# The third tile of x1n in blocks 2 to 6: turned by VectorE and memory, not by TensorE

## The chip, the core and the metric

The kernel runs on one core of one Trainium2 chip (trn2). A core has TensorE (matrix multiplications into PSUM), VectorE, ScalarE and GpSimd (elementwise work and sums), and SyncE, which here issues nearly all memory transfers. In the profile they are PE (its weight loads apart as PEld), DVE, ACT, POOL and SP. Each engine runs its own instructions in the order of the program; semaphores make one wait for another. Sixteen DMA engines carry the transfers.

The metric is the device time of one execution in microseconds (us), lower is better. A profiled execution gives a trace; its span runs from the first instruction to the last.

## The reference

A sandwich of two residual layers over x, 4 sequences of 1024 tokens with 512 features, all float32:

```python
x = x + _layernorm(_L0_attn_ref(_layernorm(x, axis=-1), Wq, Wv, Wo, Wg, ln_gamma, ln_beta, beta), axis=-1)
x = x + _layernorm(_L0_ffn_ref(_layernorm(x, axis=-1), gate_w, up_w, down_w, gate_s, up_s, down_s), axis=-1)
```

The first layer is a retention: q, v and g are projections of the normalised x (512 x 512 weights), v goes through a decaying running sum along the sequence, `out = q * ret` is normalised, scaled by `silu(g)` and projected by Wo. The second is a gated feed-forward layer with 1536 inner features, whose weights are rounded to 8-bit floats: `silu(x @ gate_w * gate_s) * (x @ up_w * up_s) @ down_w * down_s`.

Between the two stands what this change is about. x1 is x plus the first layer's normalised output; x1n is x1 normalised over its 512 features; the feed-forward layer reads x1n.

## The kernel before

**Blocks and tiles.** The 4096 tokens are cut into eight blocks (0 to 7) of 512, and a block into four tiles (s = 0 to 3) of 128 tokens. A tile has a token in each of the 128 partitions and 512 features beside each other. The feed-forward products sum over features, so for them features must lie in the partitions: each tile of x1n has to be turned (transposed). The turned block is x1nT, in two parts, because float32 values are carried as two numbers[...]: part 0 is the rounded value (`upper_of`, line 891, a copy on ACT), part 1 what is left (`rest_of`, line 894, a subtraction on VectorE).

**Two ways to turn a tile.** `turn_x1n` (875) has TensorE do it, four 128x128 pieces of a tile into one PSUM bank (`pt` in the profile). `move_x1n` (878) has VectorE turn 32x32 blocks (`xs`), writes these to DRAM in four stores of 64 KB (`mxs<-xs`) and returns a function that loads them back in exchanged places (`x1n<-mxs`, 256 KB), into the tile that x1n was in. In blocks 2 to 6, before the change, tiles 0 and 1 go through memory and tiles 2 and 3 through TensorE.

**The loop.** For block t the loop runs 12 steps (i = 0 to 11), one per 128 inner features: `f.gate(i)` and `f.up(i)` are eight matmuls each into a bank of the pair `pf` (`pfg`, `pfu`), `f.fuse(i)` multiplies the two on VectorE, and `f.down(i - 2)` sums into four banks (`pd`). Step 0's `f.gate(0)` is the first to read a block's x1nT; for its first chunk of features its first matmul reads part 0 of all four tiles and its second matmul part 1.

Into these steps the same loop weaves the first layer of later blocks: `f` is the feed-forward of block t, `b` the retention of block t + 1, `n` that of block t + 2, and `l` the feed-forward of block t - 1. `fast` holds from block 2 on for `b`. `n` exists for t = 1 to 5, so with `b` = blocks 2 to 6. In `b`'s last steps each tile goes through:

- `o_moments(s)`: mean and variance of the output projection in PSUM (`po`), VectorE; then the inverse root by GpSimd (`rstd_in_place`).
- `x1_of(s)` (852): three activations on ACT normalise it into x1n's tile, GpSimd adds it to x, SP stores the sum as `kept`.
- `x1_moments(s)` (863): the same statistics of x1; `x1n_of(s)` then normalises into x1n's tile.

Tiles 0 and 1 come early: x1_of in step 8, the moments and x1n in step 9. Tiles 2 and 3 have x1_of and their moments in step 10, and are turned in step 11.

**The projections of the next block.** `n.gap(...)` works off the passes of `n`'s v, q and g. Each pass multiplies by one 256 KB unit of weights from a ring of four (`w_ring`), and after a pass `fetch_weights` (418) has SP load the unit that comes four later. `n.gap(-2)` and `n.gap(-1)` in step 11 stand on both sides of the turns: the first starts v's chunk 0 (`begin`: two passes), the second ends it (the third pass, then a scan on VectorE) and starts chunk 1.

**What sets the order.** Every operation is issued through `InOrder` (67), which keeps the program's order on each engine; so in the profile nearly all work has line 75. SP's transfers stand in one queue, in the order of their calls. In the built program a transfer also waits for the one eight places before it on SP, as they share eight semaphores in turn.

Of the kernel before, what the change touches and what calls it, by code (L numbers as in the profile page):

```python
# [23 lines left out]
def sandwich(  # L24
# [298 lines left out]
    class Splitter:  # L323
# [34 lines left out]
        def load(self, k):  # L358

            w = wpool.tile([P, NC, D], F32R, tag=f"w{k}_sb", name=f"w{k}_units")  # L360
            for c in range(NC):
                sp.dma_start(w.bitcast(F32)[:, :, ts(c, P)], self.by_chunk(operands[k, c]["top"]))
            self.raw[k] = w
# [659 lines left out]
    b = Retention(1)  # L1023
# [177 lines left out]
    for t in range(NB):  # L1201
        f, n = Ffn(a), None
        fast = b is not None and b.fast
        for i in range(NI):
            if t > 0 and (t > 1 or i) and not (fast and i == 11):
                (f if i else l).rest((i - 1) % NI)
            if t == 0 and i == 0:
                n = Retention(2)

            if t > 0 and b and i == 0 and t < NB - 2:  # L1210
                n = Retention(t + 2)
# [81 lines left out]
                    n.diff_of(0)  # L1293
                    n.diff_of(1)
            if fast and i == 10:
                b.x1_of(2)
                b.x1_of(3)
            f.up(i)
            if n and i == 11:
                n.gap(-2)  # L1300
            if fast and i == 11:
                b.new_x1nT()
            f.fuse(i)
# [5 lines left out]
            if t == 0 and i == 9:  # L1309
                load = b.move_x1n(2)  # L1310
# [8 lines left out]
            if fast and i == 9:  # L1319
                b.o_moments(2)  # L1320
                loads = [b.move_x1n(s) for s in range(2)]
            if fast and i == 11:
                for s in range(2):
                    b.upper_of(s)
                    b.rest_of(s)
# [48 lines left out]
                n.diff_of(0)  # L1374
                n.diff_of(1)
            if fast and i == 10:
                b.x1_moments(2)
                b.x1_moments(3)
                b.x1n_of(2)
                if n:  # L1380
                    n.diff_of(2)
                    n.diff_of(3)
# [48 lines left out]
                f.down(NI - 2)  # L1431

            if n and i == 11:
                if t:
                    b.turn_x1n(2, "pf")
                    b.upper_of(2)
                    b.rest_of(2)
                b.turn_x1n(3, "pf")
                b.upper_of(3)
                b.rest_of(3)  # L1440
            if fast and i < 3:
                b.gap(3 * i + 2)
            if fast and i in (7, 8):
# [30 lines left out]
        l, a, b = f, b, n  # L1474
# [58 lines left out]
@with_exitstack  # L1533
def retention_ffn_sandwich(ctx: ExitStack, tc: tile.TileContext, *args):


    nc = tc.nc
    out, seq = args[-2:]
    kept = ctx.enter_context(tc.tile_pool(name="flag", bufs=1, space=bass.MemoryType.DRAM))
    flag = kept.tile([1, 1], I32, tag="flag", name="flag")  # L1540
    sandwich(tc, *args, flag=flag)
    beyond = nc.values_load(flag, min_val=0, max_val=0x7F800000)
    with tc.If(beyond != 0):
        with tc.tile_pool(name="rounded", bufs=1, space=bass.MemoryType.DRAM) as kept_rounded:
            weights = round_exactly(tc, kept_rounded, args[8:11], ("gate_w8", "up_w8", "down_w8"))
            sandwich(tc, *args[:8], *weights, *args[11:])
# [44 lines left out]
```

## Time and profile before

| | |
|---|---|
| median of 3 runs | 914.72 us (914.65 to 915.25) |
| the profiled execution, as a run | 913.0 us |
| its span | 911.2 us |
| VectorE busy | 631.3 us, 69% |
| ScalarE busy | 419.0 us, 46% |
| GpSimd busy | 241.4 us, 26% |
| transfers of SP's queue | 151.18 MB, 54.7% of what 16 DMA engines could be busy |
| granted clock of TensorE | 0.992 |

A busy share is an average over the span; what limits the kernel in one stretch is read from the timeline of that stretch. In the rows of a timeline stand the start, the length, the engine, the operation with what it writes and reads, and how many such instructions were merged; in square brackets, if there is one, the idle time before it and what ended it. A matmul's shown length holds its way through the array, so matmuls overlap: eight in a row begin 1.73 us after the eight before them. For a transfer the trace shows when SP issued it and how long it took to land.

### The profile page before, as it was taken

The page shows a single profiled execution, that of the slowest core. Times are in us where ns is not written, and L with a number is a line of the kernel's source. Part 1 is how long each engine was busy: PE and PEld are TensorE (multiplying, and loading weights), DVE is VectorE, ACT ScalarE, POOL GpSimd, SP SyncE. Part 2 cuts the span into 40 slices and gives each one's busy share as a digit, 9 for nine tenths or more (in the row PEclk, how much of TensorE's full clock was granted, in tenths as well). Part 3 has the DMA queues.
Part 4 walks back from the last instruction along what each step waited for, and adds up shares of the span by engine and source line. Part 5 has one row for each costly group of instructions (what it writes and reads, how often), then busy time and mean ns, then how long its engine had stood idle before and what let it go on. Part 6 is the DMA issues. An engine that isn't in the chain of part 4 may idle for free.

```text
span 911.2 us, 11999 instructions
## 1 busy us (share of the span) xinstructions
PE 884.0 (97%) x3948; PEld 741.0 (81%) x3948; DVE 631.3 (69%) x1071; ACT 419.0 (46%) x741; POOL 241.4 (26%) x304
## 2 busy tenths in 40 slices
PE   9999999989899999999999999999999999999995
PEld 7466777677688888888888888888888888888885
DVE  4888686667778684886668766786848855665545
ACT  1368556523454336443464534543364433644223
POOL 1214231301414214250332305142142503322030
PEclk9999999999999999999999999999999999999998
DMA  9964544666563775646745666627756464423021
GB/s 285 301 211 165 174 136 151 169 223 210 161 171 76 244 228 161 162 127 211 240 148 131 188 209 212 179 60 243 229 161 162 125 212 149 144 88 115 1 94 50
DMA packets 115579, 152.69 MB, mean 168 GB/s; under 512 B 10867, under 2 KB 54644, under 8 KB 115444
## 3 DMA queue, kind: packets, MB, share of 16 engines
q1 hardware_dynamic: 114644, 151.18, 54.7%
q10 hardware_dynamic: 864, 0.66, 0.3%
q8 instruction: 33, 0.54, 0.2%
q14 instruction: 38, 0.31, 0.1%
HBM read 117.46 MB, written 38.54 MB: 171 GB/s over the span
## 4 chain that ended last, share of the span: by engine, by line
PE 85%; DVE 7%; ACT 3%; DMA 2%; issue 1%; POOL 1%; DVEq 0%; SPq 0%; ACTq 0%; POOLq 0%
PE pfu L75 17%; PE pfg L75 16%; PE pd L75 15%; PE pg L75 9%; PE po L75 9%; PE pv L75 9%; PE pq L75 8%; DVE st L75 1%; DVE y L75 1%; PE idle L75 1%; DVE gate L75 1%; DMA x<-in_x 1%; PE var L75 1%; PE mu L75 1%; PE pt L75 1%
## 5 line engine op out<-in xcount | busy, mean ns | idle before, releaser
L75 PE MATMUL pfg<-x1nT,gate_sb 128*128 128x512 f32 x768 | 184.0, 382 | 1.6 <-ACT gate L75 1.5
L75 PE MATMUL pfu<-x1nT,up_sb 128*128 128x512 f32 x768 | 183.2, 381 | 0.9 <-DVE gate L75 0.9
L75 PE MATMUL pd<-down_sb,fuse 128*128 128x512 f32 x720 | 170.5, 379 | 0.0
L75 PEld LDWEIGHTS pfg<-x1nT,gate_sb 128*128 128x128 f32 x768 | 145.6, 191 | 24.8 <-ACT gate L75 3.9
L75 PEld LDWEIGHTS pfu<-x1nT,up_sb 128*128 128x128 f32 x768 | 145.0, 189 | 23.6 <-issue 1.9
L75 PEld LDWEIGHTS pd<-down_sb,fuse 128*128 128x128 f32 x720 | 141.3, 196 | 14.6
L75 ACT CAST fuse<-gate 128x512 fp32r<-128x512 f32 x90 | 55.6, 618 | 137.5 <-DVE gate L75 134.0
L75 DVE SCALAR_TENSOR_TENSOR gate<-pfu,us_sb,gate 128x512 f32<-128x512 f32 x96 | 71.7, 747 | 66.2 <-PE pfu L75 56.7
L75 ACT ACTIVATE gate<-pfg,gs_sb 128x512 f32<-128x512 f32 x96 | 65.6, 683 | 92.2 <-PE pfg L75 92.2
L75 POOL TENSOR_SCALAR mv<-mv 128x1 f32<-128x1 f32 (+1 forms) x82 | 23.0, 280 | 314.5 <-DVE mv L75 312.5
L75 DVE TENSOR_TENSOR fuse<-gate,fuse 128x512 fp32r<-128x512 f32 x90 | 71.0, 789 | 5.0 <-ACT fuse L75 4.8
L75 POOL TENSOR_TENSOR d<-d,x 128x512 f32<-128x512 f32 x28 | 41.7, 1511 | 89.6 <-ACT d L75 75.7
L75 DVE BATCH_NORM_STATS2 st<-x 128x6 f32<-128x512 f32 x64 | 43.6, 681 | 22.3 <-POOL x L75 17.3
L75 POOL TENSOR_TENSOR mv<-mv,nhalf 128x1 f32<-128x1 f32 (+1 forms) x75 | 52.2, 697 | 6.3
L75 POOL TENSOR_TENSOR x<-x,x1n 128x512 f32<-128x512 f32 x32 | 45.5, 1427 | 22.8 <-ACT x1n L75 15.8
L75 ACT ACTIVATE pv<-pv 128x512 f32<-128x512 f32 x28 | 16.3, 582 | 50.0 <-PE pv L75 50.0
L75 POOL TENSOR_TENSOR ysum<-y 128x512 f32<-128x512 f32 x8 | 10.6, 1324 | 105.1 <-DVE y L75 105.1
L75 POOL TENSOR_TENSOR sqsum<-sqsum,sq 128x512 f32<-128x512 f32 x24 | 33.7, 1404 | 17.4 <-ACT sq L75 10.1
L75 DVE TENSOR_TENSOR y<-pq,y 128x512 f32<-128x512 f32 x28 | 19.1, 682 | 22.7 <-PE pq L75 22.7
L75 DVE BATCH_NORM_STATS2 st<-po 128x6 f32<-128x512 f32 x32 | 21.9, 685 | 14.9 <-PE po L75 14.7
L75 DVE SCALAR_TENSOR_TENSOR y<-y,lnb_sb,mids 128x512 f32<-128x512 f32 x28 | 27.0, 965 | 7.1 <-ACT mids L75 7.0
L75 ACT ACT_TABLE_LOAD x19 | 24.4, 1283 | 16.3 <-DVE var L75 12.2
(214 smaller groups left out, 1488.9 us busy)
## 6 DMA issues: line engine op xcount, KB each, us to landing
x<-in_x SPq DMA_DIRECT2D x52, 256.0 KB, 5.4
kept<-x SPq DMA_DIRECT2D x32, 256.0 KB, 3.2
x<-kept SPq DMA_DIRECT2D x32, 256.0 KB, 4.3
out<-d SPq DMA_DIRECT2D x31, 256.0 KB, 2.0
w_ring<-dtop_v SPq DMA_DIRECT2D x24, 256.0 KB, 3.3
w_ring<-dlow_v SPq DMA_DIRECT2D x24, 256.0 KB, 3.4
w_ring<-ddiff_v SPq DMA_DIRECT2D x24, 256.0 KB, 3.5
w_ring<-dtop_q SPq DMA_DIRECT2D x24, 256.0 KB, 2.6
```

The source lines that it names most:

```text
L75: return lambda *args, **kwargs: tc.keep_in_program_order(op(*args, **kwargs))
```

## The change

In blocks 2 to 6 tile 2 takes the way of tiles 0 and 1. Its x1_of moves from step 10 to step 9, its x1_moments from behind `f.fuse(10)` to ahead of `f.up(10)`, and x1n_of(2) from behind x1_moments(3) to ahead of it; after that `move_x1n(2)` is called in step 10, and its load in step 11 behind `n.gap(-2)`. In step 11 tile 3 is now the only one that TensorE turns, and tile 2's upper_of and rest_of come after tile 3's. In block 7 (where there is no `n`) only x1n_of(2) changes places with x1_moments(3). No operation is new: all of them were in the kernel before for other tiles.

```diff
             if fast and i == 10:
-                b.x1_of(2)
+                if n:
+                    b.x1_moments(2)
+                else:
+                    b.x1_of(2)
                 b.x1_of(3)
             f.up(i)
             if n and i == 11:
                 n.gap(-2)
+                if t:
+                    load()
             if fast and i == 11:
                 b.new_x1nT()
             f.fuse(i)
...
             if fast and i == 9:
                 b.o_moments(2)
                 loads = [b.move_x1n(s) for s in range(2)]
+                if n:
+                    b.x1_of(2)
...
             if fast and i == 10:
-                b.x1_moments(2)
+                if not n:
+                    b.x1_moments(2)
+                b.x1n_of(2)
+                if n:
+                    load = b.move_x1n(2)
                 b.x1_moments(3)
-                b.x1n_of(2)
                 if n:
                     n.diff_of(2)
                     n.diff_of(3)
...
             if n and i == 11:
-                if t:
-                    b.turn_x1n(2, "pf")
-                    b.upper_of(2)
-                    b.rest_of(2)
                 b.turn_x1n(3, "pf")
                 b.upper_of(3)
                 b.rest_of(3)
+                if t:
+                    b.upper_of(2)
+                    b.rest_of(2)
```

## The prediction

> **What bounds the kernel now.** I read the page first, then TensorE's timeline around the turn of one block into the next, then SP's timeline over the same stretch, then what its transfers took to land.
>
> ```profile
> span 911.2 us, 11999 instructions
> PE 884.0 (97%) x3948; PEld 741.0 (81%) x3948; DVE 631.3 (69%) x1071; ACT 419.0 (46%) x741; POOL 241.4 (26%) x304
> PE 85%; DVE 7%; ACT 3%; DMA 2%; issue 1%; POOL 1%; DVEq 0%; SPq 0%; ACTq 0%; POOLq 0%
> ```
>
> TensorE is busy 97% of the span and is 85% of the chain that ended last. Each of its instructions that goes shortens the kernel, as long as TensorE finds its operands in time. So I need the slack of the operands at the place of the change. TensorE there (block 2, start and length in us):
>
> ```profile
> 303.38 1.89 PE L75 MATMUL pd<-down_sb,fuse 128*128 128x512 f32 x8
> 305.11 1.04 PE L75 MATMUL pt<-ident,x1n 128*128 128x128 f32 x8
> 305.90 1.11 PE L75 MATMUL pv<-diff,w_ring 128*128 128x512 f32 x4
> 306.85 1.03 PE L75 MATMUL pv<-xnT,w_ring 128*128 128x512 f32 x4
> 307.71 1.03 PE L75 MATMUL pv<-low,w_ring 128*128 128x512 f32 x4
> 308.57 1.89 PE L75 MATMUL pfg<-x1nT,gate_sb 128*128 128x512 f32 x8
> ```
>
> There is no gap. The eight `pt` are the turns of tiles 2 and 3. At 308.57 `pfg` starts: step 0 of the next Ffn and the first reader of all of x1nT. SP's issues over that stretch:
>
> ```profile
> 292.91 3.73 SPq L75 DMA_DIRECT2D mxs<-xs  x8
> 296.73 0.39 SPq L75 DMA_DIRECT2D w_ring<-dtop_v  x1
> 297.22 0.40 SPq L75 DMA_DIRECT2D w_ring<-dlow_v  x1
> 297.71 0.38 SPq L75 DMA_DIRECT2D w_ring<-ddiff_v  x1
> 298.19 0.38 SPq L75 DMA_DIRECT2D w_ring<-dtop_v  x1
> 298.66 0.87 SPq L75 DMA_DIRECT2D x1n<-mxs  x2
> 299.58 0.91 SPq L75 DMA_DIRECT2D kept<-x  x2
> 302.71 0.32 SPq L75 DMA_DIRECT2D w_ring<-dlow_v  x1
> 303.57 0.32 SPq L75 DMA_DIRECT2D w_ring<-ddiff_v  x1
> ```
>
> and the DMA engines by stretch (the two numbers at the end of a row are their busy share and GB/s), with how long the two kept stores at 299.6 and 300.1 took to land:
>
> ```profile
> 296.70:298.20 1.50, 1.50 (x9) 1.35 (x7) 0.75 (x1) 1.34 (x4) 1.20 (x1) 1.00 0.67 133
> 298.20:305.70 7.50, 7.50 (x39) 6.65 (x38) 5.62 (x11) 3.47 (x7) 3.40 (x6) 1.00 0.98 318
> 306.50:308.00 1.50, 1.50 (x9) 1.31 (x8) 1.50 (x4) 0.33 (x1) 0.00 (x0) 1.00 0.01 3
> ...
> L75 SPq DMA_DIRECT2D kept<-x x2: 426/430/434, 299.6 to 300.1; - x2
> ...
> DMA to landing us min/median/max: 5.4/5.5/5.6
> ```
>
> From 298.2 to 305.7 the DMA engines are full (0.98), and what SP issues at 300.05 lands only at about 305.7. The change sends a tile out and back through just this stretch.
>
> **What the Trainium skill says.** (1) "VectorE: DVE Perf Modes", The three transpose paths: VectorE turns only 32x32 blocks, TensorE a whole 128x128. The trace agrees in that tiles 0 and 1 need one STREAM_TRANSPOSE (median 678 ns) and then a trip through memory to exchange blocks. (2) "DMA: Bandwidth & Descriptors", Anatomy of one DMA: about 2.0 us fixed plus bytes over 436 GB/s, so an estimate of 2.6 us for 256 KB. The shortest x1n<-mxs here took 2.6 us (issue at 828.0) and another 2.7 (170.9); the median was 5.0. (3) Same page, Queues, rings and completion order: on a DMA engine descriptors are consumed in ring order. The trace agrees: four 64 KB stores issued at 160 to 161.5 behind loads took 4.2 to 4.7 us to land, while an idle queue took 1.8. (4) Same page, Two DMAs through the same engine are not ordered: a DMA that reads what another wrote must be issued after the wait for its semaphore; SP waits "DMA mxs<-xs" here for 6.7 us in all.
>
> **The change part by part**, for one block; times are those of block 2.
>
> *Removed.* Four transposes and one PSUM bank of the `pf` pair. The eight `pt` with four `pv` take 306.85 - 305.11 = 1.74 us; four matmuls take 4 x 0.216 = 0.86 (1.73 us per group of eight), so eight turns cost 0.88 and four 0.44. Five blocks (2 to 6): 2.2 us at most. The built program's order confirms 20 turns fewer.
>
> *Moved, x1_of(2) to step 9.* Its mean and rstd are ready at 293.2 (POOL), so ACT can run its three activations by 294.4 instead of 296.9. It is in time before gate(10) at 294.95 on ACT. POOL's sum follows (1.28 us, to about 295.7), and now stands ahead of o_moments(3)'s rstd, which ends at 296.6 against 295.6. x1_of(3) needs that one and starts its last two activations at 296.65 against 297.25 before: no loss. On SP its kept store now stands right after the eight mxs, before four w_ring loads and both x1n loads: each issues about 0.48 later and lands one 256 KB transfer (about 0.7 us) later. dlow_v is read at 302.3 and landed at 297.2 + 3.2 = 300.4: covered. If it were not, its delay would be swallowed by the later wait below.
>
> *Moved on VectorE.* st of x1(2) goes before fuse(10): x is there at 295.7, st and aggr end at 296.6, and pfu ends at 296.7. x1n_of(2) runs behind it (rstd from POOL 297.4) at 297.5 to 298.1, the new STREAM_TRANSPOSE (0.68) to 298.8. VectorE idles from 297.5 to 298.3 and 299.0 to 299.7 in the profile, which hides them. gate(11) at 302.3 stays in place: nothing on the path, at most 0.2 us a block without that cover. In block 7 (no n) only x1n_of(2) moves ahead of x1_moments(3): 0 to 0.3 us once; I take 0.
>
> *Added, the trip.* In the built program SP now issues: 8 mxs, kept 2, 4 w_ring, 2 x1n, kept 3, 4 mxs of tile 2, w_ring dlow_v and ddiff_v, then x1n(2)'s load, which waits until those four stores have landed. SP's transfers also each wait for the eighth one before; the fourth store waits for ddiff_v (297.7 + 4.6 = 302.3 before, one transfer later now, about 303). None of that binds before the queue does:
> - kept 3 lands where it did, since the same eight transfers stand in the full stretch: at 300.1 + 5.6 = 305.7.
> - The four stores land behind it. At 160 to 161.5 such stores, behind a load that landed at 159.4 + 5.1 = 164.5, landed 0.2 us apart, the third at 160.9 + 4.2 = 165.1, so the fourth at about 165.3 (its landing is not in the trace): +0.85, here 306.55.
> - SP issues the load (0.1) and it takes 2.65: 309.3.
> - ACT's upper_of(2) 0.62, then VectorE's rest_of(2) 0.69, with about 0.05 to start each. pfg's first matmul needs the first, its second (the loop takes both parts of a chunk in turn) the second; a weight load of 0.2 stands ahead of each. The second matmul starts at 309.3 + 1.66 = 310.96, and 7 x 0.216 end the group's stream at 312.5. Before it ended at 308.57 + 1.73 = 310.3. Loss 2.2 us, with the saved 0.44 already swallowed, as the start is now set by the tile and not by TensorE.
>
> With L the landing, the loss is L - start of pfg + 1.44, and L = last kept landing + 3.6. For the five blocks kept 3 lands 2.9, 2.3, 2.9, 3.2 and 1.7 us before pfg (pfg at 308.57, 414.63, 520.59, 627.60, 733.60; block 4's second landing is estimated from its first). Mean 2.58: loss 3.6 - 2.58 + 1.44 = 2.46 us, five times 12.3.
>
> *Who stands behind the new waits.* ACT: pv's scaling, used after pfg, so no further loss. VectorE: the scans of v0, 1.5 us, and rest(11); v0's bank is wanted again after pfu, some 3 us later. SP: the next w_ring dtop_v, issued at 307.04 before, now about 306.9, and in_x, not urgent. No one carries the delay further, nor do the lost microseconds come back, since TensorE has no gaps to give: in 306 to 410 it is busy 103.99 of 104.
>
> Sum against the profiled execution: 911.2 + 12.3 = 923.5 us of span. It took 913.0 as a run, 1.7 under the median 914.7; the median becomes 914.7 + 12.3 = 927.0.
>
> Bounds of the trip. Low: the stores overtake the queue; the fourth, issued at 303.1, lands 1.8 later at 304.9, L is 307.65, loss 0.5 a block, 917.3. High: the full stretch grows by another slow transfer as block 6's does (6.7 us to land), loss 3.5 to 3.7 in each, 933. I take the middle, because landings in order are what this trace shows.
>
> **The rivals.**
> - *The tile is back in time.* Then 20 turns go and nothing else: 914.7 - 2.2 = 912.5, faster. For it: tiles 0 and 1 do the trip today without a stall, and the DMA engines are nearly idle (0.01) from 306.5 to 308. Against it: pfg could then start at 308.13, so the tile must land by 306.7 for the whole gain (306.7 + 1.66 is its second matmul) and by 308.57 - 1.44 = 307.1 for any; the stores would have to be in by 304.4, before kept 3 is. It decides from L = 307.1 downwards.
> - *The queue is shorter than counted,* because kept 2 leaves earlier: stores in by 305.6, loss 1.5, 5 x 1.5 = 7.5: 922.2, slower still. It decides if the full stretch ends a transfer or more earlier.
> - *A longer queue,* as in the high bound, w_ring loads pushed too: 933.
> - *The change doesn't do what it says:* excluded by the order of the built program.
>
> **How the numbers follow.** My forecast (loss of 2 to 3 a block) 0.55, shorter queue 0.22, longer 0.14, in time 0.06, and 0.03 for a stop where gain and loss cancel. About 0.2% is what a measurement of this kernel can tell from no change. Range: from 918, near the low bound, to 933, the high one; it leaves out the faster case and a little beyond each end. Faster 0.06, same 0.03, slower 0.91.
>
> **What would show it.** Right: `pt` x48 instead of x68; pfg of step 0 waiting 1.5 us or more behind ACT or VectorE on x1nT in each of blocks 2 to 6 and nowhere else; upper_of(2) idle until "DMA x1n<-mxs"; x1n(2)'s load issued only at about 306.6 in block 2's clock. Wrong: no idle time of TensorE there, or the third tile's stores landing within 2 us of issue while kept 3 is still out.

## The result, and the profile after

| | before | changed |
|---|---|---|
| median | 914.23 us (6 runs) | 929.40 us (6 runs, 927.92 to 931.32) |
| ratio, 95% interval | | 1.0174 (1.0157 to 1.0191) |
| span of the profiled execution | 911.2 us | 926.3 us |

The change costs 15.2 us; 12.3 were forecast. The first lines of the changed kernel's page, and the shares of its chain of waits:

```profile
span 926.3 us, 12008 instructions
PE 889.9 (96%) x3928; PEld 741.7 (80%) x3928; DVE 635.7 (69%) x1076; ACT 419.3 (45%) x741; POOL 242.9 (26%) x304
PE 73%; DVE 9%; DMA 7%; ACT 4%; POOL 3%; issue 2%; SPq 1%; DVEq 0%; POOLq 0%; ACTq 0%
```

TensorE has 20 instructions fewer (3928 for 3948; `pt` is x48), yet is busy 5.9 us longer. The span grew by 15.1: so it stands idle for 9.2 us more, and does its work more slowly for the rest. The chain has gone from TensorE (85% to 73%) to the transfers (2% to 7%). The waits of TensorE from 300 to 800 us in the changed kernel (in all, times, longest; for the kernel before this view has one line, `pq`, 0.8 us):

```profile
PE pfg L75 <- ACT x1nT L75: 8.4, 5, 1.9
PE pfg L75 <- DVE x1nT L75: 1.0, 4, 0.2
PE pv L75 <- DMA w_ring<-dlow_v: 0.8, 3, 0.3
...
```

One long wait a block, on the copy of part 0; in four of the five a short one on part 1; and in three one that was not forecast, on v's low weights. TensorE's timeline at the turn of block 2 in the changed kernel:

```profile
305.29 0.60 PE L75 MATMUL pt<-ident,x1n 128*128 128x128 f32 x4
305.65 1.11 PE L75 MATMUL pv<-diff,w_ring 128*128 128x512 f32 x4
306.60 1.03 PE L75 MATMUL pv<-xnT,w_ring 128*128 128x512 f32 x4
307.83 1.13 PE L75 MATMUL pv<-low,w_ring 128*128 128x512 f32 x4 [0.20 <-DMA w_ring<-dlow_v]
310.70 0.48 PE L75 MATMUL pfg<-x1nT,gate_sb 128*128 128x512 f32 x1 [1.75 <-ACT x1nT L75]
311.43 1.78 PE L75 MATMUL pfg<-x1nT,gate_sb 128*128 128x512 f32 x7 [0.24 <-DVE x1nT L75]
```

Eight `pt` have become four, and `pfg` starts at 310.70 instead of 308.57. SP's timeline there:

```profile
300.23 0.43 SPq L75 DMA_DIRECT2D kept<-x  x1
300.77 2.59 SPq L75 DMA_DIRECT2D mxs<-xs  x4
303.99 0.34 SPq L75 DMA_DIRECT2D w_ring<-dlow_v  x1
304.76 0.34 SPq L75 DMA_DIRECT2D w_ring<-ddiff_v  x1
307.32 0.32 SPq L75 DMA_DIRECT2D x1n<-mxs  x1
```

and the chain of waits from 300 to 315 us, in order of time (start, length, what):

```profile
298.38 4.65 DMA w_ring<-ddiff_v
...
303.05 4.08 DMA mxs<-xs
...
307.32 2.69 DMA x1n<-mxs
...
310.03 0.63 ACT x1nT L75
...
310.68 0.70 DVE x1nT L75
...
311.43 1.78 PE pfg L75 x7
```

Read from the bottom, this is the mechanism whole: the second matmul waits for part 1, this for part 0, this for the tile's load (2.69 us), and this for the last of four stores, which needed 4.08 us for 64 KB. This store was issued only when the transfer eight places before it (`ddiff_v`) had landed, but that did not set its landing: the stores landed at 306.38, 306.70, 306.93 and 307.13, 0.2 to 0.3 apart and all behind the second kept store (306.12), although they were issued over 2.3 us. What they waited for is what stood ahead of them, not their own issue.

Where the loss arises is read from the starts of the same instructions in both traces. Later than before by, in us:

| at (clock of before) | 300 | 400 | 500 | 610 | 720 | 850 |
|---|---|---|---|---|---|---|
| changed kernel | +0.19 | +3.14 | +5.81 | +8.49 | +10.71 | +14.72 |

From just before the turns to the end of the first `pfg`, blocks 2 to 6 lose 2.6, 2.7, 3.7, 1.9 and 4.0 us. Between the turns the start of `pq` shifts by +0.4, -1.1 and +0.4 us (at 337, 550 and 656): the kernel before waits 0.79 us there at 550 and the changed one does not, so a little comes back. By item, over the five: turns gone -2.2; v's low pass +1.5; start of `pfg` +9.7; its second matmul +0.6 each in three blocks, but +1.9 and +2.1 in blocks 4 and 6 (14.8; the shifts between the turns take 0.3 back). Those two carry something that is not a wait. The stretches around the five starts of `pfg` (stretch, length, then busy time and count of PE, PEld, DVE, ACT and POOL, then TensorE's granted clock, DMA share, GB/s):

```profile
310.00:313.50 3.50, 2.55 (x11) 2.02 (x12) 2.75 (x5) 1.36 (x3) 0.00 (x0) 1.00 0.94 302
419.00:422.50 3.50, 2.44 (x10) 1.93 (x11) 2.63 (x5) 1.24 (x3) 0.00 (x0) 1.00 0.97 296
527.50:531.50 4.00, 3.32 (x7) 2.43 (x8) 2.85 (x5) 1.10 (x2) 0.00 (x0) 0.59 0.99 330
637.00:640.00 3.00, 2.41 (x10) 1.90 (x11) 2.61 (x5) 0.89 (x3) 0.00 (x0) 1.00 0.94 313
745.50:750.00 4.50, 3.53 (x8) 2.70 (x9) 2.85 (x5) 1.10 (x2) 0.00 (x0) 0.63 0.88 308
```

and TensorE's timeline at block 4's turn:

```profile
528.18 3.83 PE L75 MATMUL pfg<-x1nT,gate_sb 128*128 128x512 f32 x8 [1.54 <-ACT x1nT L75]
531.84 1.03 PE L75 MATMUL pv<-diff,w_ring 128*128 128x512 f32 x4
```

Around the turns of blocks 4 and 6 the mean granted clock is 0.59 and 0.63, not 1.00, and at block 4's turn eight `pfg` take 531.84 - 528.18 = 3.66 us, not 1.73. After the wait TensorE runs its first 3.4 us at half speed. The Trainium skill has this: "TensorE: Matmul & The Clock Gate", Part 1, What's actually happening, tells of two clock states, full and half, the lower after an idle window of about 3.4 us. The trace agrees in the two states, but here idles of 1.54 and 1.88 us were enough; the kernel before has no such stretch between 300 and 800.

Which waits bring the half clock can be read from the traces. In the changed kernel, from 60 to 890 us, half-clock stretches begin at 115.19, 203.93, 248.31, 528.20 and 746.65 us. Each lasts 3.41 us, and the starts lie 26, 13, 82 and 64 times 3.413 us apart. In every profile of this case that has more than one, they are whole multiples of 3.413 us apart too: the stretches keep to a fixed grid. In the piece of the grid just before its stretch, TensorE did nothing for 1.78 us in block 4 (524.79 to 528.20) and 1.88 in block 6 (743.24 to 746.65). In blocks 2 and 3 a line of the grid, at 309.75 and 418.97, cuts the wait in two, and no piece holds more than 1.21 us of idling; block 5's whole wait lies in one piece, but is only 1.52. Over all profiles in this range, the 37 pieces before a slow stretch hold 1.67 to 2.61 us of idling; no piece with less than 1.67 was followed by one, and of those between 1.67 and 1.96 eight were not.

### The profile page after: what moved, and what is told of

Read it like the earlier page. It is cut to its first block, busy times and chain, and to the rows that moved or that the text cites. A ratio compares the mean times of both kernels' runs of the same rounds, so it can differ in the third digit from the quotient of the medians.

```text
span 926.3 us, 12008 instructions
## 1 busy us (share of the span) xinstructions
PE 889.9 (96%) x3928; PEld 741.7 (80%) x3928; DVE 635.7 (69%) x1076; ACT 419.3 (45%) x741; POOL 242.9 (26%) x304
## 4 chain that ended last, share of the span: by engine, by line
PE 73%; DVE 9%; DMA 7%; ACT 4%; POOL 3%; issue 2%; SPq 1%; DVEq 0%; POOLq 0%; ACTq 0%
PE pfg L75 14%; PE pfu L75 14%; PE pd L75 12%; PE pg L75 9%; PE po L75 8%; PE pq L75 8%; PE pv L75 6%; DVE st L75 2%; DMA mxs<-xs 2%; DMA w_ring<-ddiff_v 2%; DMA x1n<-mxs 2%; DVE y L75 1%; POOL x L75 1%; SPq L75 1%; POOL mv L75 1%
## 5 line engine op out<-in xcount | busy, mean ns | idle before, releaser
L75 PE MATMUL pfg<-x1nT,gate_sb 128*128 128x512 f32 x768 | 189.6, 389 | 11.1 <-ACT x1nT L75 8.4
L75 PEld LDWEIGHTS pfg<-x1nT,gate_sb 128*128 128x128 f32 x768 | 147.8, 194 | 38.4 <-ACT x1nT L75 10.4
L75 POOL TENSOR_TENSOR x<-x,x1n 128x512 f32<-128x512 f32 x32 | 48.1, 1510 | 22.4 <-ACT x1n L75 21.0
```

The lines of the kernel that those rows point to most:

```text
L75: return lambda *args, **kwargs: tc.keep_in_program_order(op(*args, **kwargs))
```

## The experiments

**Theory:** the tile is late because its four stores and then its load stand behind a full queue; what else was moved is free. **Rival A:** the moved work on VectorE, ScalarE and GpSimd costs too. **Rival B:** five more transfers (four stores and a load) in a full stretch slow everything, whatever reads them. Unless said otherwise, an edit is against the changed kernel, and the kernel of before ran beside each.

**1. The moves without the trip.** TensorE turns tile 2 again, ahead of tile 3; all else of the change stays.

```diff
-                if t:
-                    load()
...
-                if n:
-                    load = b.move_x1n(2)
...
             if n and i == 11:
-                b.turn_x1n(3, "pf")
-                b.upper_of(3)
-                b.rest_of(3)
                 if t:
+                    b.turn_x1n(2, "pf")
                     b.upper_of(2)
                     b.rest_of(2)
+                b.turn_x1n(3, "pf")
+                b.upper_of(3)
+                b.rest_of(3)
```

> The moves of tile 2's sum, moments and x1n stay as in the change, but TensorE turns the tile as before and nothing goes through memory. Theory (the tile's landing behind a full transfer queue costs the time): TensorE never waits on x1nT at the first gate matmul of a block, 914 to 915 us, ratio 0.999 to 1.002. Rival 1 (the moved work on ScalarE, VectorE and GpSimd is late): keeps a large part of the loss, 920 us or more.

Measured: 913.54 us, before 913.32, ratio 1.0007 (0.9997 to 1.0016). Rival A falls.

**2. The trip without a reader.** All added transfers and VectorE's turn stay, but the load goes into VectorE's turn buffer, which nothing reads; TensorE turns the tile. The output is computed in full.

```diff
-                    load = b.move_x1n(2)
+                    load = b.copy_x1n(2)
...
+        def copy_x1n(self, s):
...
+            return lambda: sp.dma_start(t, m)
```

> The change with all its added transfers (VectorE's turn, four stores and the load at the same places of the queue), but the load goes into the buffer of VectorE's turn, which nobody reads, and TensorE turns the tile as before. Theory: the wait goes with the reader; up to 0.4 us a block stay where the ring's weights come later behind the stores (v's second pass), 914 to 917 us. Rival 2 (the added 512 KB a block slow the weights of the ring, whoever reads the tile): 922 us or more.

Measured: 915.00 us, ratio 1.0021 (1.0005 to 1.0036). The traffic by itself costs about 0.2%: TensorE waits, from 300 to 800 us of this kernel's profile:

```profile
PE pv L75 <- DMA w_ring<-dlow_v: 0.5, 2, 0.3
...
PE pv L75 <- DMA w_ring<-dtop_v: 0.3, 1, 0.3
```

So rival B has a small part, through the ring's weights; the rest, about seven eighths of the loss, needs the reader.

**3. Less ahead of the stores.** If the queue sets the landing, each 256 KB taken from ahead of the stores must bring the tile nearer. First both kept stores (2 and 3), then only the later one, go behind the tile's load.

```diff
-            sp.dma_start(self.kept[s], x)
+            if not (self.fast and self.t < NB - 1 and s in (2, 3)):
+                self.keep(s)
...
                     load()
+                    b.keep(2)
+                    b.keep(3)
```

> The change, with the kept stores of tiles 2 and 3 behind the third tile's load in SP's queue: two 256 KB transfers fewer ahead of its stores. Theory: stores and load land 2 x 0.7 = 1.4 us earlier in each block, the loss falls from 2.5 to about 1.1 us a block, and no TensorE idle time there is long enough for a half-clock stretch: 918 to 921 us. Rival 3 (the round trip itself is too long from VectorE's turn on, whatever stands ahead): stays at 927 us or more.

> The change with only tile 3's kept store behind the third tile's load: one 256 KB transfer fewer ahead of its stores. Theory: 0.7 us a block less than the change, half of what both late kept stores give, and one or no half-clock stretch: ratio 1.010 to 1.0145, between the change (1.0174) and both late (1.0072). Rival 3 (what stands ahead does not matter): 1.016 or more.

Measured: both late 919.84 us, 1.0072 (1.0051 to 1.0094); only the later one 923.27 against 912.89, 1.0107 (1.0083 to 1.0131). With both late, SP and then TensorE's wait from 300 to 800 us:

```profile
299.58 1.91 SPq L75 DMA_DIRECT2D mxs<-xs  x4
...
305.41 0.32 SPq L75 DMA_DIRECT2D x1n<-mxs  x1
```
```profile
PE pfg L75 <- ACT x1nT L75: 5.6, 5, 1.8
```

The load is issued at 305.41, not 307.32, and the wait falls from 8.4 to 5.6 us (6.4 with one store late). The ratios fall in the order that the theory asks for: 1.0174, 1.0107, 1.0072. It also asks for equal steps; these are 0.67% and 0.35%, and the intervals of the last two runs overlap. Not foreseen was a half-clock stretch that stays in block 3 (`pfg` waits 1.80 us there), and two with one store late, so the ratios mix the queue with the clock.

**4. More out of the way.** As in 3 with both stores late; then v's fourth ring load of step 9 goes behind the tile's stores, and the tile's load ahead of `n.gap(-2)`, so that v's low and difference weights come after it.

```diff
-                if part == "diff" and s == NS - 1:
+                if part == "diff" and s == NS - 1 and (c < NC - 1 or self.t == NB - 1):
...
-                n.gap(-2)
                 if t:
                     load()
+                n.gap(-2)
...
                     load = b.move_x1n(2)
+                    fetch_weights()
```

> As the kernel with late kept stores, and in addition the fourth ring load of step 9 goes behind the third tile's stores, and the tile's load is called ahead of the two ring loads of step 11. Theory: stores in by about 303, the load issued at once and landed by about 306 (in block 2's clock), before TensorE is through: no wait on x1nT, the 20 turns are saved, 911 to 913 us, ratio about 0.998. Rival 3: still a wait at the first gate matmul, above 914.5 us.

Measured: 916.18 us, 1.0035 (1.0021 to 1.0049); a miss. TensorE's waits from 300 to 800 us:

```profile
PE pv L75 <- DMA w_ring<-dlow_v: 1.6, 3, 0.7
...
PE pv L75 <- DMA w_ring<-dtop_v: 0.6, 1, 0.6
```

The wait on x1nT is gone, as the theory has it. But SP stood at the load, which waits for the stores, until 304.88, and v's low weights behind it were issued at 305.33 and landed at 308.51. What stands behind a waiting transfer is late too.

**5. Half the clock.** The changed kernel with eight more matmuls ahead of the first `pfg` of each of the five blocks, into the same bank, which the first real matmul then overwrites. They keep TensorE busy while the tile is awaited.

```diff
+            if i == 0 and 2 <= self.t < NB - 1:
+                for _ in range(8):
+                    pe.matmul(pg, mean_r, gate_sb[:, 0, :TB], start=True, stop=True)
             project(pg, gate_sb, i, self.parts)
```

> The change, with eight extra matmuls (8 x 0.216 = 1.7 us, result overwritten) ahead of the first gate group of blocks 2 to 6, where TensorE waits for the third tile anyway. Theory (the part of the loss above 12.3 us comes from stretches of half clock that follow an idle TensorE): no half-clock stretch at any of the five places, the wait itself as long as before, ratio 1.012 to 1.0145 against 1.0174 of the change. Rival 4 (the rest of the loss comes from something else): ratio as the change or above.

Measured: 925.48 us, before 914.66, 1.0122 (1.0095 to 1.0148). More work, and 0.5% less time than the change. TensorE there in block 4, and the stretches (clock third from the end):

```profile
523.98 2.02 PE L75 MATMUL pfg<-gate_sb,mean_r 128*128 128x512 f32 x8
525.87 0.48 PE L75 MATMUL pfg<-x1nT,gate_sb 128*128 128x512 f32 x1
526.60 1.78 PE L75 MATMUL pfg<-x1nT,gate_sb 128*128 128x512 f32 x7 [0.24 <-DVE x1nT L75]
```
```profile
527.50:531.50 4.00, 4.00 (x21) 3.49 (x20) 3.30 (x7) 0.69 (x1) 0.00 (x0) 1.00 0.81 291
```

`pfg` goes at full speed. Its profile has no half-clock stretch at any of the five turns. From 300 to 850 us this kernel falls back by 12.6 us (from -2.36 to +10.27 against before) where the change falls back by 14.5. So about 2 us of the loss are the slow clock in that one profile, and up to 4.7 by the medians (1.0174 - 1.0122), whose intervals leave some 2 to 7.5: how often an execution meets such a stretch is not known.

**6. The second matmul.** The changed kernel, with the first gate group of these blocks running part 0 of all four chunks ahead of part 1.

```diff
+        order = [(c, h) for c in range(NC) for h in range(len(parts))]
+        if by_part:
+            order.sort(key=lambda ch: ch[1])
```

> The change, with the first gate group of blocks 2 to 6 in the order part 0 of all four chunks, then part 1. Theory (the second matmul's wait for rest_of(2) is worth about 0.5 to 0.6 us a block in the change): 5 x 0.55 = 2.7 us less than the change, ratio 1.0125 to 1.015. Rival 5 (the tile's two parts are not what the group waits for): no difference to the change, 1.016 or more.

Measured: 923.23 us, 1.0105 (1.0075 to 1.0135), below the expected 1.0125 to 1.015, into which the interval reaches. The short wait on part 1 is gone and the long one is not (8.3 us, 5 times); this profile has one half-clock stretch at a block's turn, not two. In its profile the loss from 300 to 850 us is 10.8. How much of the gain is the order of the parts and how much one slow stretch fewer was not separated.

**7. The tile's stores first of all.** As in 4 with kept stores late, but the tile's four stores go ahead of the loads of tiles 0 and 1, and its load between the two ring loads of step 11; once alone, once with the order of 6.

```diff
-                for load in loads:
-                    load()
+                if not n:
+                    for load in loads:
+                        load()
...
                     load = b.move_x1n(2)
+                    for first in loads:
+                        first()
+                    fetch_weights()
```

> Late kept stores, and the third tile's four stores ahead of the loads of tiles 0 and 1, the fourth ring load behind those, and the third tile's load between the two ring loads of step 11 (so that v's low weights no longer stand behind the load's wait). Theory (place in SP's queue decides): the ring wait of the kernel before this one goes, the tile lands at about 306.7 in block 2's clock, just in time: ratio 0.998 to 1.000, 911.5 to 914 us. Rival 3 (the round trip is too long whatever the order): still 1.003 or more.

> The same, and the first gate group of blocks 2 to 6 runs through part 0 of all four chunks before part 1, so that the tile's subtraction on VectorE has four matmuls (0.86 us) more time. Theory: if the tile is only just late, this hides it: ratio 0.997 to 0.999, 911 to 913 us, no wait on x1nT. Rival 3: a wait for ScalarE's copy of part 0 remains.

Measured: 920.23 us, 1.0050 (1.0029 to 1.0071), and 917.65, 1.0030 (1.0018 to 1.0042); both misses. In the first, waits of 300 to 800 us:

```profile
PE pv L75 <- DMA w_ring<-dlow_v: 1.7, 2, 1.4
PE pv L75 <- DMA w_ring<-dtop_v: 1.4, 3, 0.8
...
PE pfg L75 <- ACT x1nT L75: 0.9, 2, 0.8
```

The tile is nearly in time, but now v's top weights, issued at 301.91, landed at 306.73. The place in the queue was taken from them. The profiled execution (923.13 us) was the slowest of the seven, with a half-clock stretch at block 5's turn, so its waits stand for more than the median.

**8. Another queue.** Kept stores late, and ScalarE issues the tile's stores and its load, this ahead of `n.gap(-2)`; once alone, once with the order of 6.

```diff
-                    load = b.move_x1n(2)
+                    load = b.move_x1n(2, act)
```

> The change with late kept stores, and the third tile's four stores and its load issued by ScalarE instead of SP, the load between gate(11) and the scaling of v, where ScalarE idles. Theory (the tile stands behind other transfers of SP's queue, and its wait there blocks the ring loads): on a queue of its own the stores land by about 302 to 303 and the tile by about 306 in block 2's clock, and no ring load waits for it; the 20 turns are saved: 911 to 914 us, ratio 0.997 to 1.000. Rival (the DMA engines' total capacity in the full stretch is what lacks, whichever queue): ring loads or the tile are late all the same, ratio 1.002 or more.

> The same, with the first gate group through part 0 of all chunks before part 1. Theory: if the tile is in time without it, no difference, 0.997 to 0.999; if the tile is late by up to half a microsecond, it hides that. Rival (capacity): 1.001 or more, with waits on the ring.

Measured: 925.16 us, 1.0122 (1.0099 to 1.0144), and 922.93, 1.0107 (1.0087 to 1.0127), against 912.89; both far off. SP's wait from 297 to 303 us, SP's issues, and TensorE's largest wait from 300 to 800, in the first:

```profile
SPq L75 <- DMA mxs<-xs: 3.8, 1, 3.8
```
```profile
297.62 0.38 SPq L75 DMA_DIRECT2D w_ring<-dtop_v  x1
301.83 0.81 SPq L75 DMA_DIRECT2D x1n<-mxs  x2
302.75 0.36 SPq L75 DMA_DIRECT2D w_ring<-dlow_v  x1
```
```profile
PE pv L75 <- DMA w_ring<-dlow_v: 9.5, 5, 2.3
```

The queues are not independent. In the built program the rule of the eighth transfer before counts both engines' transfers together, so SP's load of tile 0 now waits 3.8 us for a store of ScalarE's and is issued at 301.83, not 298.66. v's low weights are issued about when they were (302.75; 302.71 before), but now close behind the loads of all three tiles, and landed at 308.83 instead of 306.28; the load of tile 2 took 6.2 us. Three of the five turns also have a half-clock stretch. A transfer that isn't tied so was not tried, so whether the engines' capacity alone would make a second queue useless stays open here.

**9. Each reader served in its order.** As in 4, but the tile's load stands between v's low and v's difference weights, and the order of 6.

```diff
             if n and i == 11:
-                n.gap(-2)
                 if t:
-                    load()
+                    n.begin("v", 0, "pa0", load)
+                    b.keep(2)
+                    b.keep(3)
+                else:
+                    n.gap(-2)
```

> Orders that keep the third tile on VectorE: the stores of kept tiles 2 and 3 go to the end of the stretch, the fourth ring load of step 9 is issued behind the third tile's stores, the third tile's load between the two ring loads of step 11 (so v's low weights are issued ahead of it), and the first gate group runs its first part for all chunks ahead of its second. Theory (each reader was late only because of what stood ahead of it on SP's queue): the low weights are issued at about 303 of block 2 and land by 306, the load is issued at about 305 and lands at about 307.5, the first half of the tile is copied by 308.2, just as TensorE comes to it: 912.5 to 914.5, ratio 0.998 to 1.001, no wait over 0.3 us a block on the ring or on x1nT. Rival (the stretch has no room for eight more transfers in any order): 1.002 or more, with a wait of 0.4 us a block or more on one of the ring's weights or on the tile.

Measured: 914.36 us, before 913.39, ratio 1.0004 (0.9991 to 1.0016). SP and TensorE in block 2:

```profile
302.04 0.34 SPq L75 DMA_DIRECT2D w_ring<-dlow_v  x1
304.31 0.32 SPq L75 DMA_DIRECT2D x1n<-mxs  x1
304.73 0.38 SPq L75 DMA_DIRECT2D w_ring<-ddiff_v  x1
305.16 0.90 SPq L75 DMA_DIRECT2D kept<-x  x2
```
```profile
306.60 1.03 PE L75 MATMUL pv<-low,w_ring 128*128 128x512 f32 x4
307.73 1.99 PE L75 MATMUL pfg<-x1nT,gate_sb 128*128 128x512 f32 x8
```

The low weights landed at 305.27, the tile at 307.03, and neither the `pv` passes ahead of it nor `pfg` shows a wait at block 2's turn. Over 300 to 800 us 1.6 us of waits on x1nT remain (1.19 in block 3, 0.43 in block 4), 0.7 on v's top weights (at 317.35) and 1.0 on `pq`. So the loss of 1.74% is a matter of SP's order and of the order of two parts, not of VectorE's turning as such: the ratio came out where the theory put it, its bound of 0.3 us a block did not hold in blocks 3 and 4. Which of the two orders gave how much of the step from experiment 4 was not separated. What is left of the 2.2 us saved goes in those waits. No version ran measurably faster than the kernel before.

## Why the prediction was right, and where it was off

- *TensorE is the bound, and its operand's slack decides:* held. In the changed kernel each of the five blocks has the long wait on part 0 of x1nT (1.52 to 1.88 us), and no other place has one.
- *20 turns gone, swallowed by the wait:* held; -0.44 us a block shows in the starts until `pfg`.
- *The moved work costs nothing:* held (experiment 1, +0.07%, interval over zero).
- *The stores land behind kept 3, 0.2 apart; the load is issued then:* held, with small misses. In before's clock kept 3 landed at 305.9 (forecast 305.7), the fourth store 1.0 later (0.85), the load was issued 0.2 later (0.1) and took 2.69 (2.65): landing at 309.8 instead of 309.3. That the queue is the cause was shown by experiments 3 and 9.
- *From landing to the second matmul 1.66 us:* it took 1.42, so most of this miss was given back: the second matmul came at 311.24 in before's clock against 310.96. By block the rule gave 2.1, 2.7, 2.1, 1.8 and 3.3 us; the turns lost 2.6, 2.7, 3.7, 1.9 and 4.0.
- *What is queued behind the waits:* mostly right. Not foreseen were v's low weights, late by 1.5 us over the five blocks. With the change this adds nothing, as the tile sets `pfg`'s start; where the tile is not awaited, experiment 2 prices the added traffic at about 0.2%. That TensorE has no gaps to give was read from 306 to 410 us alone: at 550 it had one of 0.79 us, and 1.1 us came back there, most of which `pq`'s shifts at 337 and 656 take away again.
- *The sum:* 12.3 us forecast, 15.2 measured. What the sum lacks is a term: after a wait TensorE ran at half clock in blocks 4 and 6, 1.3 and 1.5 us more than the same step in the other blocks, 2.8 together. With this taken off, the turns lost 2.6, 2.7, 2.4, 1.9 and 2.5 us, 12.0 together; that this is so near the rule's sum is in part luck, as block 2 lost 0.4 more than the rule says and block 6 0.8 less. Without slow stretches (experiment 5) the profile falls back by 12.6. How many of them an execution meets depends on where the waits fall in the grid of 3.413 us, which the prediction did not count.
- *The rivals:* "in time" needs the tile by 307.1 in before's clock; it landed at 309.8. Experiment 9 comes near it (307.7 in that clock, with the order of parts asking for less), yet without its gain. "Shorter queue" did not occur; 929.4 lies in the range, between forecast and "longer queue", but most of the surplus in this profile is the clock's, not the queue's.

## What to carry to other kernels

Work that leaves the busiest engine for memory is priced by when it comes back: look up the first reader, count what stands ahead in the queue of each leg of the trip, and compare with the reader's start. In a stretch whose transfers are full, room for one is taken from another, so list every reader of that stretch and order the queue by their times; a load that waits for its own stores also holds back all that is behind it. And a wait on a full TensorE costs more than its length if the clock drops after it.

## What was not expected of the hardware

- The clock halved after short waits, and by a fixed grid: 1.54 us in block 4 and 1.88 in block 6 brought it, 1.75 and 1.74 in blocks 2 and 3 did not. In the first two the piece of 3.413 us before the stretch held 1.78 and 1.88 us of idling, in the others at most 1.21. Where the grid lies against a kernel's start differs from profile to profile, so the same wait can cost more in one execution than in another.
- A store of 64 KB issued into the full stretch took 4.1 to 5.6 us to land, and two queues of different engines did not part the traffic; here the program ties their transfers together (SP waited 3.8 us).
